# Two adaLN layers on one core: key blocks summed by VectorE ahead of the softmax sums, and a reordered schedule

## The chip, the core and the metric

The kernel runs on one core of a Trainium2 chip. TensorE (PE) does the matrix products, VectorE (DVE), ScalarE (ACT) and GpSimd (POOL) work on tiles, and SyncE (SP) mostly issues DMAs. Each engine has a queue of its own, works through it in order and meets the others through semaphores. The metric is the device time of one execution in microseconds: 575.76 us before, the median of three runs (573.43 to 576.96).

## The reference

Eight batches of 256 tokens with 128 channels go through two layers. Each layer is attention and then a routed feed-forward network, both with a layer norm whose scale and shift come from a small modulation product, and a gate on the way back into the residual:

```
h = _layernorm(x) * (1 + ca) + sa;   x = x + ga * attention(h)
h = _layernorm(x) * (1 + cb) + sb;   x = x + gb * ffn(h)
```

Layer 1, where nearly all of the change lies, has causal attention with 16 heads of width 64. The softmax needs, for each query and head, the sum of the exponentials over the keys. Its feed-forward part has 16 experts with an inner width of 64: sigmoid of the router logits, the best two of each token weighted by their share, and a shared expert besides:

```
out  = einsum('bhst,bhtv->bhsv', softmax(masked / sqrt(64)), v)
ffn  = x + mlp_shared(x) + sum over the two chosen experts of value * mlp_expert(x)
```

## The kernel before

`fast_path` writes every engine's order out by hand. Layer 0 comes first (24 steps of attention, then its experts), then layer 1.

**The loop of layer 1** (L2101 to L2123) has 32 units, four per batch, four heads per unit. Unit n has, in this order: the scores of unit n (L1660), the q and k projections for unit n+2 (L1633), the steps registered for the middle (`at`, list `early`), the value products of unit n-1 (L1681), the v projection for unit n+2 (L1645), and the steps registered for the end (`at_end`, list `ends`). A third list (`at_head`) puts steps between the four heads of the scores. Other work, such as norms, routing, output projections and gathers, is spread over the units through these lists.

**Attention.** A unit's exponentials lie in two tiles `pt` of two heads each, 128 keys by 384 columns: columns 0 to 255 are all 256 queries against the first 128 keys, columns 256 to 383 the second 128 queries against the second 128 keys. ACT makes the exponentials, POOL clears the triangle above the diagonal in four instructions (`causal`, L820), and PE multiplies by v into `o` (L1692). A second group of products (L1700) sums over the keys: its weight is a matrix of ones that sends each head to its own row of `sum`, and it streams all 384 columns, block 0 and then block 1. DVE copies `o` out (L1704). After a batch's last unit DVE takes the reciprocal (L1708), SP sends it through DRAM (`rd`) and back spread over partitions (`rb`), and two units later `normalise1` multiplies (L1725) and `finish1` projects (L1745). The last batch has no such trip: `spread_last` (L1727) spreads the reciprocals with PE.

**Routing.** The rows of the first 12 of the 16 token tiles are scattered by POOL into a sorted DRAM buffer `xs`, in which each of 16 experts has a region. The buffer is cleared first: `z1.clear` (L889) is one DMA of 12 MB, at the end of unit 8. A scatter waits until the buffer is clear (L943). When all rows are placed, `tables_steps` (L956) works out which tile of rows belongs to which expert. Its first step is one small PE product (`cnt`) and fourteen DVE instructions, the last of which gives `widx`, the weights' indices; it runs at the end of unit 29. SP reads these indices into registers and issues the loads: `fetch_weights1` (L1843, groups 4 and up), `find_rows1` (L1839), `fetch_rows1` (L1826). Groups 0 to 3 have fixed places and need no table. The loads of groups 4 and up do.

**After the loop** the ten groups of four tiles go through `turn1` (transpose, L1865), `hidden1` (L1875) and `project_tiles` (L1888), in an order written out from L2128 on. `turn1(m)` issues the rows of group m+4. `project_tiles` leaves its result in two PSUM tiles, which DVE copies to `ysb` (L1899), and SP stores. The PSUM tiles of all this have tags: "s" (two), "o" and "sum" (one each), and "p", which is what `ps_ln` hands out. When the last store has landed, POOL gathers each token's two rows (L1058), and `combine1` adds them, weighted, with PE (L2018). The last 512 tokens instead go densely through all experts (`dense_hidden`, `dense_gate`, `dense_project`), which fills the time of the gathers. `add_h` (L1771, called `add` in the schedule) adds the gated tokens to x on POOL.

Of the kernel before, what the change touches and what calls it, by code (L numbers as in the profile page):

```python
# [9 lines left out]
F32 = mybir.dt.float32  # L10
# [3 lines left out]
ALU = mybir.AluOpType  # L14
AX = mybir.AxisListType

P = 128
# [540 lines left out]
def fast_path(ctx: ExitStack, tc: tile.TileContext, i: dict, out: bass.AP, bad: bass.AP):  # L558
# [302 lines left out]
    class Sorted:  # L861


        def __init__(self, pool, tag, ne, nt, nd):
            self.pool, self.tag, self.ne, self.nt, self.nd = pool, tag, ne, nt, nd
            self.cap = cap = nt * P
            self.placed = 0
            self.scatters = []
            f32 = lambda shape, name: pool.tile(shape, F32, name=f"{name}{tag}")
            self.s12 = f32([P, nt, 2, ne], "s12")  # L870
            self.slot = f32([P, nt, 2], "slot")
            self.region = f32([P, ne], "region")

            self.seen = pool.tile([P, nt + 1, ne], BF16, name=f"seen{tag}")
            self.yidx = pool.tile([P, nt, 2], I32, name=f"yidx{tag}")
            self.rowi = pool.tile([P, nd], I32, name=f"rowi{tag}")
            self.widx = pool.tile([P, nd], I32, name=f"widx{tag}")
            self.xs = dram.tile([ne * cap, P], F32, name=f"xs{tag}")
            self.ys = dram.tile([(ne + nd) * P, P], F32, name=f"ys{tag}")
            nc.gpsimd.tensor_scalar(self.region, num[:, :ne], float(cap), 0.0, ALU.mult, ALU.add)  # L880
            nc.gpsimd.memset(self.seen[:, 0, :], 0.0)
            self.marks = [pool.tile([P, 7, ne], BF16, name=f"marks{tag}{n}") for n in range(E1 // ne)]
            for t in self.marks:
                nc.gpsimd.memset(t[:, 0:3, :], 0.0)
# [1 line left out]
        def tmp(self, shape, name, dt=F32, bufs=2):  # L886
            return self.pool.tile(shape, dt, tag=name, bufs=bufs, name=f"{name}{self.tag}_{self.n}")

        def clear(self, zero):  # L889
            m = zero.shape[1]  # L890
            self.fill = nc.sync.dma_start(
                out=self.xs.rearrange("(p a) c -> p (a c)", p=P).rearrange("p (n m) -> p n m", m=m),
                in_=zero.unsqueeze(1).to_broadcast([P, self.ne * self.cap // m, m]),
            ).ins

        def place(self, *args):
            for _ in self.place_steps(*args):
# [39 lines left out]
        def apart(self, ins):  # L937


            group = f"scatters{self.tag}"  # L940
            if self.scatters:
                tc.declare_no_dep(ins, group=group, reason="different rows")
                tc.add_manual_dep(ins, self.fill.name, WAIT, reason="rows are cleared first")  # L943
            tc.add_to_no_dep_group(group, ins)
            self.scatters.append(ins)

# [445 lines left out]
    def at_end(n, *steps):  # L1392
        ends.setdefault(n, []).extend(steps)
# [66 lines left out]
    first_gates, last_gates = one(gates0(0, 8)), one(gates0(8, 8))  # L1460
    at_end(17, first_gates)
    at_end(18, first_gates)
    at_end(20, first_gates)
    norm6, norm7 = norm0(SPANS0[4]), norm0(SPANS0[5])
    at_end(22, lambda: turn_gates0(0))
    at_end(23, norm6[0], lambda: turn_gates0(1), lambda: ways[SPANS0[3]]())
# [193 lines left out]
    def scores1(b, u, between):  # L1660

        q, k = st1.pop(("q", b, u)), st1.pop(("k", b, u))
        for m in range(2):
# [14 lines left out]
                    step()  # L1678
            st1["pt", b, c] = pt

    def values1(b, u):  # L1681
        v = st1["v", b, u // 2]
        if u == 0:
            st1["s", b] = pp.tile([P, S], F32, tag="sum", bufs=1, name=f"sum1_{b}")
            st1["ou", b] = lp.tile([P, 2, 4, S], F32, tag="ou", name=f"ou1_{b}")
        s = st1["s", b]
        o = pp.tile([P, 2, S], F32, tag="o", bufs=1, name=f"o1_{b}_{u}")
        pts = [st1.pop(("pt", b, 2 * u + m)) for m in range(2)]
        for m in range(2):
            for kb, cols, qs in blocks:  # L1690
                for n in range(2):
                    nc.tensor.matmul(  # L1692
                        out=o[bass.ts(n, D1), m, qs], lhsT=v[:, kb, bass.ts(4 * (u % 2) + 2 * m + n, D1)],
                        rhs=pts[m][:, n, cols], start=(kb == 0), stop=(kb == 1), skip_group_check=True,
                    )

        for kb, cols, qs in blocks:
            for m in range(2):
                for n in range(2):
                    nc.tensor.matmul(  # L1700
                        out=s[bass.ts(2 * n + m, 32), qs], lhsT=on[:, u, :], rhs=pts[m][:, n, cols],
                        start=(kb == 0 and u == 0), stop=(kb == 1 and u == 3), skip_group_check=True,
                    )
        nc.vector.tensor_copy(st1["ou", b][:, :, u, :], o)  # L1704

# [21 lines left out]
    def spread_last(us):  # L1727

        aT = st1["ou", B - 1]
        for u in us:  # L1730
            rp = pp.tile([P, 2, S], F32, tag="s", name=f"rp1_{u}")
            for m in range(2):
                nc.tensor.matmul(
                    out=rp[:, m, :], lhsT=sel[:, u, m].rearrange("p n d -> p (n d)"), rhs=st1["r", B - 1],
                    start=True, stop=True,
                )
            nc.vector.tensor_tensor(aT[:, :, u, :], aT[:, :, u, :], rp, ALU.mult)
# [101 lines left out]
    def find_rows1(m):  # L1839

        starts.extend(z1.row_starts(4 * m - E1, 4))
# [46 lines left out]
    def project_tiles(m):  # L1888
        a = sq.pop(("a", m))
        y = [pp.tile([P, 2, P], F32, tag=tag, bufs=1, name=f"yq1_{m}_{tag}") for tag in ("o", "sum")]  # L1890
        for t in range(4):
            k = t % 2
            nc.tensor.matmul(
                out=y[k][:, t // 2, :], lhsT=a[bass.ts(k, I1), t // 2, :], rhs=weights1(m, t)[2],
                start=True, stop=True,
            )
        ysb = lp.tile([P, 2, 2, P], F32, tag="ysb", bufs=3, name=f"ysb1_{m}")
        for k in range(2):
            nc.vector.tensor_copy(ysb[:, :, k, :], y[k])  # L1899
        nc.sync.dma_start(  # L1900
            out=z1.ys[bass.ds(4 * m * P, 4 * P), :].rearrange("(t p) c -> p t c", p=P),
            in_=ysb.rearrange("p a k c -> p (a k) c"),
        )
# [172 lines left out]
    for bs in ((0, 2), (2, 2), (4, 1), (5, 1)):  # L2076
        n = 4 * sum(bs) + 2
        measure, normalise, modulate, tokens, add = norm1(bs)
        go = one(route1(bs))
        at_end(n, measure)  # L2080
        at(n + 1, normalise)
        at_end(n + 1, modulate, tokens)
        at(n + 2, go)
        at_end(n + 2, go, go, go, go)
        if bs[0] < 5:
            at(n + 4, go)
        else:
            at_end(n + 3, go)
        for k in range(4 * bs[1]):
            if bs[0] < 5:  # L2090
                at_head(n + 5 + k // 2, 1 + 2 * (k % 2), go)
            else:
                at_head(n + 4, 3, lambda go=go: scatter(go, 1))
        if bs[0] < 5:
            at_end(n + 4 if bs[0] else n + 7, add)
    tables = one(z1.tables_steps(ps_ln, True))
    at_end(29, tables, lambda: fetch_weights1(4), lambda: fetch_weights1(5))
    at_end(30, *[lambda m=m: fetch_rows1(m) for m in range(4)], *[lambda m=m: find_rows1(m) for m in range(4, NQ)],
          lambda: fetch_weights1(6))

    for n in range(N):  # L2101
        b, u = divmod(n, 4)
        scores1(b, u, behind.pop(n, {}))
        if n == 0:
            nc.gpsimd.memset(sel, 0.0)
            nc.gpsimd.affine_select(
                out=sel, in_=sel, compare_op=ALU.not_equal, fill=1.0, base=0,
                pattern=[[-8, 4], [-32, 2], [-64, 2], [0, D1]], channel_multiplier=1,
            )
        if n + 2 < N:  # L2110
            project_qk1(*divmod(n + 2, 4))
        for step in early.pop(n, ()):
            step()
        if n:
            values1(*divmod(n - 1, 4))
        if n + 2 < N:
            project_v1(*divmod(n + 2, 4))
        if u == 0 and b:
            reciprocals1(b - 1)
            if b == 2:  # L2120
                z1.clear(zero1)
        for step in ends.pop(n, ()):
            step()  # L2123

# [79 lines left out]
    shared_project(2)  # L2204
    dense_hidden(2)
    dense_hidden(3)
    dense_gate(0)
    dense_hidden(4)
    dense_gate(1)
    dense_hidden(5)  # L2210
    dense_gate(2)
    combine1(0, 1, 2, 3)
    ffn1_add(0)
    dense_hidden(6)
    dense_gate(3)
    dense_project(0)
    dense_project(1)
    dense_hidden(7)
    dense_gate(4)
    combine1(4)  # L2220
    dense_project(2)
    dense_gate(5)
    dense_project(3)
    combine1(5)
    dense_gate(6)
    dense_project(4)
    combine1(6, 7)
    dense_gate(7)
    ffn1_add(1)
    dense_project(5)  # L2230
    combine1(8)
    dense_project(6)
    combine1(9)
    dense_project(7)
    combine1(10, 11)
    ffn1_add(LAST)
    ffn1_add(2)
    manual.close()
    l1.close()
# [94 lines left out]
```

## Time and profile before

| What | Value |
|---|---|
| Runs, median (lowest, highest) | 575.76 us (573.43, 576.96) |
| The profiled execution, own time | 605.03 us |
| Its span, first to last instruction | 603.2 us |
| PE busy, share of the span | 543.5 us, 90% |
| DVE, ACT, POOL busy | 323.8, 265.5, 265.2 us |
| Loop of layer 1 on PE | 239.4 to 493.5 us |
| Granted PE clock, mean | 0.965 |

All times inside the kernel are microseconds from the start of the span of this one profiled execution. It took 29.3 us longer than the median run. Between 545 and 572 us nearly everything but the gathers stands still in it, with waits whose releaser the profile cannot name. "Busy" says little of what bounds a stage. For that one looks at what an engine waited for, and at the chain of work that ended last.

### The profile page before, as it was taken

The numbers are of one execution on the slowest core, as the hardware profiler recorded it, in microseconds if no ns is written. First come the engines' busy times: TensorE is split into PE (matmuls) and PEld (weight loads), VectorE is DVE, ScalarE is ACT, GpSimd is POOL, SyncE is SP. The second block draws the span as 40 slices with busy tenths as digits, with TensorE's granted clock in tenths as the row PEclk, the third lists the DMA queues.
The fourth block names the chain that finished last, engine by engine and source line by source line (L and its number), as shares of the span: only waits on it lengthen the run. The fifth ranks groups of instructions, "written<-read, shape, count | busy, mean of one in ns | idle before, by whom it ended". The sixth has DMA issues, their size and how long they took to land.

```text
span 603.2 us, 12004 instructions
## 1 busy us (share of the span) xinstructions
PE 543.5 (90%) x4499; PEld 384.4 (64%) x4499; DVE 323.8 (54%) x988; ACT 265.5 (44%) x495; POOL 265.2 (44%) x404
## 2 busy tenths in 40 slices
PE   5999998889999998999999989999999989885194
PEld 4355554468999986666767666766767677742064
DVE  4258886666422224655366646558374757771143
ACT  3678775244556633653344423462534322262010
POOL 5224576574444123855123525333563440647400
PEclk9999999799999999999999999999999999987688
DMA  8699100315999713104069831203030355555101
GB/s 278 243 399 406 56 19 27 129 44 155 327 342 354 238 39 153 36 18 99 1 211 408 326 72 46 60 3 71 14 93 10 82 175 170 166 148 131 36 19 57
DMA packets 53566, 85.40 MB, mean 142 GB/s; under 512 B 6652, under 2 KB 32764, under 8 KB 52348
## 3 DMA queue, kind: packets, MB, share of 16 engines
q1 hardware_dynamic: 45308, 60.50, 31.3%
q0 software_dynamic: 8048, 23.67, 12.1%
q8 instruction: 37, 0.61, 0.4%
q10 hardware_dynamic: 144, 0.39, 0.2%
q14 instruction: 29, 0.24, 0.1%
HBM read 53.46 MB, written 31.07 MB: 140 GB/s over the span
## 4 chain that ended last, share of the span: by engine, by line
PE 68%; DVE 12%; DMA 6%; ACT 5%; issue 3%; another core or an unknown queue 3%; SPq 1%; POOL 0%; DVEq 0%; ACTq 0%; POOLq 0%
PE sc L1670 6%; PE hp L1351 6%; PE yt L1359 6%; PE sc L1120 5%; PE o L1692 5%; PE qp L1639 5%; PE y L1745 5%; PE kp L1639 4%; PE vp L1652 4%; PE o L1154 3%; PE sum L1700 3%; DMA rb<-rd 2%; PE gud L1942 2%; DVE ou L1725 2%
## 5 line engine op out<-in xcount | busy, mean ns | idle before, releaser
L822 POOL TENSOR_SCALAR_AFFINE_SELECT pt<-pt 128x256 f32<-128x256 f32 (+1 forms) x144 | 67.1, 494 | 153.8 <-ACT pt L1673 118.3
L1058 POOL DMA_INDIRECT yg<-ys,yidx x56 | 53.9, 963 | 40.7 <-issue 20.5
L1673 ACT ACTIVATE pt<-sc 128x768 f32<-128x768 f32 x64 | 48.4, 808 | 31.2 <-PE sc L1670 31.1
L1136 ACT ACTIVATE pt<-sc 128x1024 f32<-128x1024 f32 x48 | 46.7, 1026 | 24.6 <-PE sc L1120 11.7
L1670 PEld LDWEIGHTS sc<-q,k 64*128 64x128 f32 x512 | 41.6, 187 | 18.7 <-issue 13.8
L1670 PE MATMUL sc<-q,k 64*128 64x256 f32 (+1 forms) x512 | 50.5, 337 | 0.0
L1353 ACT ACTIVATE hst<-hp,wt 128x128 f32<-128x128 f32 x136 | 38.8, 368 | 25.8 <-ACT hst L1353 24.2
L1692 PE MATMUL o<-pt,v 128*64 128x256 f32 (+1 forms) x512 | 48.7, 332 | 1.2 <-DVE ou L1704 1.2
L1655 ACT COPY v<-vp 128x512 f32<-128x512 f32 x32 | 18.7, 585 | 67.4 <-PE vp L1652 67.4
L1050 POOL DMA_INDIRECT wt<-in_wpk_dram,widx x31 | 29.5, 950 | 34.0 <-PE xT L1342 28.3
L1692 PEld LDWEIGHTS o<-pt,v 128*64 128x64 f32 x512 | 31.8, 136 | 18.2 <-issue 5.0
L1643 DVE COPY q<-qp 128x512 f32<-128x512 f32 x32 | 22.0, 688 | 37.3 <-PE qp L1639 37.3
L1364 DVE COPY ysb<-yt 128x128 f32<-128x128 f32 x39 | 11.3, 290 | 49.8 <-PE yt L1359 49.8
L1639 PE MATMUL qp<-h,wq 128*128 128x256 f32 x128 | 36.1, 404 | 1.7 <-DVE sh L1309 1.3
L1120 PE MATMUL sc<-qm,k 32*128 32x512 f32 x192 | 36.0, 722 | 1.4 <-ACT pt L1136 0.8
L1745 PE MATMUL y<-wo,ou 128*128 128x128 f32 x256 | 31.7, 281 | 5.9 <-DVE ou L1725 3.0
L932 POOL DMA_INDIRECT xs<-ht0b,idx x32 | 31.9, 998 | 11.2 <-issue 7.7
L1745 PEld LDWEIGHTS y<-wo,ou 128*128 128x128 f32 x256 | 29.9, 192 | 9.9 <-DVE at L922 4.6
L1652 PE MATMUL vp<-wv,h 128*128 128x512 f32 x64 | 36.0, 645 | 0.0
L1351 PE MATMUL hp<-xTs,wt 128*128 128x128 f32 x272 | 35.9, 275 | 0.0
L1359 PE MATMUL yt<-wt,hst 128*128 128x128 f32 x272 | 35.8, 275 | 0.0
L1351 PEld LDWEIGHTS hp<-xTs,wt 128*128 128x128 f32 x272 | 33.0, 192 | 0.0
(308 smaller groups left out, 1080.9 us busy)
## 6 DMA issues: line engine op xcount, KB each, us to landing
xs<-zero SPq DMA_DIRECT2D x1, 12288.0 KB
xs<-zero SPq DMA_DIRECT2D x1, 8192.0 KB
rb<-rd SPq DMA_DIRECT2D x14, 512.0 KB
mdb<-mrd SPq DMA_DIRECT2D x2, 2048.0 KB
xg<-xs SPq DMA_DIRECT2D x63, 64.0 KB
wt<-in_wpk_dram SPq DMA_DIRECT2D x24, 128.0 KB
wst<-in_wpk_dram SPq DMA_DIRECT2D x5, 514.0 KB
ys<-ysb SPq DMA_DIRECT2D x10, 256.0 KB
```

The costliest lines, as they stand in the source:

```text
L822: nc.gpsimd.affine_select(out=pt, in_=pt, compare_op=ALU.is_ge, fill=0.0, base=0, pattern=[[0, pt.shape[1]], [1, P]], channel_multiplier=-1,)
L1058: nc.gpsimd.indirect_dma_start(out=yg[:, k, :], out_offset=None, in_=self.ys[:, :], in_offset=bass.IndirectOffsetOnAxis(ap=self.yidx[:, j, ...
L1120: nc.tensor.matmul(out=sc[:, n, :].rearrange("p (a q) -> p a q", q=rhs.shape[2]), lhsT=k[r, cols], rhs=rhs, start=True, stop=u < 2,)
L1136: nc.scalar.activation(pt[:, bass.ts(half, 2), :], sc, AF.Exp)
L1351: nc.tensor.matmul(out=hp[:, c, :], lhsT=wt[:, bass.ts(c, P)], rhs=xT, start=True, stop=True)
L1359: nc.tensor.matmul(out=y, lhsT=hs[:, c, :], rhs=wt[:, bass.ds(WF + c * P, P)], start=(c == 0), stop=(c == FC - 1))
L1639: nc.tensor.matmul(out=ps_[:, n, :], lhsT=w1[f"w{what}1"][:, bass.ts(2 * u + n, P)], rhs=hb, start=True, stop=True)
L1652: nc.tensor.matmul(out=vp, lhsT=hb[:, bass.ts(j, P)], rhs=w1["wv1"][:, bass.ts(half, 512)], start=True, stop=True)
L1670: nc.tensor.matmul(out=sc[:, n, cols], lhsT=k[r, m, bass.ts(kb, P)], rhs=q[r, m, qs], start=True, stop=True)
L1673: nc.scalar.activation(pt, sc[:, :, 0:384], AF.Exp, scale=1.0 / math.sqrt(D1))
L1692: nc.tensor.matmul(out=o[bass.ts(n, D1), m, qs], lhsT=v[:, kb, bass.ts(4 * (u % 2) + 2 * m + n, D1)], rhs=pts[m][:, n, cols], start=(kb == ...
L1745: nc.tensor.matmul(out=y[:, j, :], lhsT=aT[:, c % 2, c // 2, bass.ts(j, P)], rhs=w1["wo1"][:, c, :], start=(c == 0), stop=(c == NC1 - 1),)
```

## The change

In layer 1 a new step, `add_blocks1`, follows the v projection of every unit: DVE adds the second key block's 128 columns to the same queries' columns of the first block, for both tiles of the unit. The sums then stream 128 columns of `pt` and 128 columns of the new tile, 256 in place of 384.

The rest moves work. The clearing of `xs` becomes three DMAs at the ends of units 4, 8 and 12. A gate step of layer 0 moves from the end of step 20 to that of 21. `spread_last` takes its PSUM tile from "p". ACT makes the second of the two copies in `project_tiles`. `add_h` of two spans moves a unit later. The rows of groups 0 to 3 are fetched at the end of unit 30, ahead of the tables. The tables' first step moves from the end of unit 29 to the start of unit 31's end steps, and the loads that need it follow in that unit. The dense part after the loop gets another order.

```diff
-        def clear(self, zero):
+        def clear(self, zero, part=0, parts=1):
             m = zero.shape[1]
...
+            n = self.ne * self.cap // m // parts
...
+                for fill in self.fills:
+                    tc.add_manual_dep(ins, fill.name, WAIT, reason="rows are cleared first")
...
-    at_end(20, first_gates)
+    at_end(21, first_gates)
...
+    def add_blocks1(b, u):
+
+        both = st1["both", b, u] = lp.tile([P, 2, 2, P], F32, tag="both", name=f"both1_{b}_{u}")
+        for m in range(2):
+            pt = st1["pt", b, 2 * u + m]
+            nc.vector.tensor_tensor(both[:, m], pt[:, :, P:S], pt[:, :, S : S + P], ALU.add)
...
-        for kb, cols, qs in blocks:
+        both = st1.pop(("both", b, u))
+        for j in range(2):
             for m in range(2):
                 for n in range(2):
                     nc.tensor.matmul(
-                        out=s[bass.ts(2 * n + m, 32), qs], lhsT=on[:, u, :], rhs=pts[m][:, n, cols],
-                        start=(kb == 0 and u == 0), stop=(kb == 1 and u == 3), skip_group_check=True,
+                        out=s[bass.ts(2 * n + m, 32), bass.ts(j, P)], lhsT=on[:, u, :],
+                        rhs=both[:, m, n, :] if j else pts[m][:, n, 0:P],
+                        start=(u == 0 and j == 0), stop=(u == 3), skip_group_check=True,
                     )
...
-            rp = pp.tile([P, 2, S], F32, tag="s", name=f"rp1_{u}")
+            rp = ps_ln([P, 2, S], f"rp1_{u}")
...
-        for k in range(2):
-            nc.vector.tensor_copy(ysb[:, :, k, :], y[k])
+        nc.vector.tensor_copy(ysb[:, :, 0, :], y[0])
+        nc.scalar.copy(ysb[:, :, 1, :], y[1])
...
-            at_end(n + 4 if bs[0] else n + 7, add)
+            at_end(n + 5 if bs[0] else n + 7, add)
     tables = one(z1.tables_steps(ps_ln, True))
-    at_end(29, tables, lambda: fetch_weights1(4), lambda: fetch_weights1(5))
-    at_end(30, *[lambda m=m: fetch_rows1(m) for m in range(4)], *[lambda m=m: find_rows1(m) for m in range(4, NQ)],
-          lambda: fetch_weights1(6))
+    at_end(30, *[lambda m=m: fetch_rows1(m) for m in range(4)])
+    ends[N - 1].insert(0, tables)
+    at_end(
+        N - 1, lambda: fetch_weights1(4), lambda: fetch_weights1(5),
+        *[lambda m=m: find_rows1(m) for m in range(4, NQ)], lambda: fetch_weights1(6),
+    )
...
+        add_blocks1(b, u)
         if u == 0 and b:
             reciprocals1(b - 1)
-            if b == 2:
-                z1.clear(zero1)
+            if b < 4:
+                z1.clear(zero1, b - 1, 3)
...
+    combine1(0, 1, 2, 3)
     dense_gate(0)
-    dense_hidden(4)
     dense_gate(1)
...
     dense_project(0)
     dense_project(1)
+    dense_hidden(4)
...
-    combine1(10, 11)
     ffn1_add(LAST)
+    combine1(8, 9, 10, 11)
     ffn1_add(2)
```

More of the change, by code (lines that the diff above doesn't have):

```diff
@@ L867, in __init__ @@
             self.placed = 0
-            self.scatters = []
+            self.fills, self.scatters = [], []
             f32 = lambda shape, name: pool.tile(shape, F32, name=f"{name}{tag}")
@@ L887, in tmp @@
             return self.pool.tile(shape, dt, tag=name, bufs=bufs, name=f"{name}{self.tag}_{self.n}")
-        def clear(self, zero):
+        def clear(self, zero, part=0, parts=1):
             m = zero.shape[1]
[L891 to L894, printed above, removed]
+            n = self.ne * self.cap // m // parts
+            rows = self.xs.rearrange("(p a) c -> p (a c)", p=P).rearrange("p (n m) -> p n m", m=m)
+            self.fills.append(
+                nc.sync.dma_start(
+                    out=rows[:, bass.ts(part, n), :], in_=zero.unsqueeze(1).to_broadcast([P, n, m])
+                ).ins
+            )
         def place(self, *args):
@@ L942, in apart @@
                 tc.declare_no_dep(ins, group=group, reason="different rows")
-                tc.add_manual_dep(ins, self.fill.name, WAIT, reason="rows are cleared first")
+                for fill in self.fills:
+                    tc.add_manual_dep(ins, fill.name, WAIT, reason="rows are cleared first")
             tc.add_to_no_dep_group(group, ins)
@@ L2094, in fast_path @@
         if bs[0] < 5:
-            at_end(n + 4 if bs[0] else n + 7, add)
+            at_end(n + 5 if bs[0] else n + 7, add)
     tables = one(z1.tables_steps(ps_ln, True))
-    at_end(29, tables, lambda: fetch_weights1(4), lambda: fetch_weights1(5))
-    at_end(30, *[lambda m=m: fetch_rows1(m) for m in range(4)], *[lambda m=m: find_rows1(m) for m in range(4, NQ)],
-          lambda: fetch_weights1(6))
+    at_end(30, *[lambda m=m: fetch_rows1(m) for m in range(4)])
[3 more added lines that the diff above has]
+        *[lambda m=m: find_rows1(m) for m in range(4, NQ)], lambda: fetch_weights1(6),
+    )
     for n in range(N):
@@ L2206, in fast_path @@
     dense_hidden(3)
+    combine1(0, 1, 2, 3)
     dense_gate(0)
-    dense_hidden(4)
     dense_gate(1)
[L2210 to L2215, printed above, removed]
     dense_project(0)
     dense_project(1)
+    dense_hidden(4)
+    dense_gate(2)
+    ffn1_add(0)
+    dense_project(2)
+    dense_hidden(5)
+    dense_gate(3)
+    dense_project(3)
+    dense_hidden(6)
+    dense_gate(4)
+    dense_project(4)
     dense_hidden(7)
-    dense_gate(4)
-    combine1(4)
-    dense_project(2)
     dense_gate(5)
-    dense_project(3)
-    combine1(5)
+    dense_project(5)
+    combine1(4, 5)
     dense_gate(6)
-    dense_project(4)
+    dense_project(6)
     combine1(6, 7)
@@ L2229, in fast_path @@
     ffn1_add(1)
[L2230 to L2233, printed above, removed]
     dense_project(7)
-    combine1(10, 11)
     ffn1_add(LAST)
+    combine1(8, 9, 10, 11)
     ffn1_add(2)
```

## The prediction

> **What bounds the kernel now.** I read the page first, then the stretches, then PE's waits.
>
> ```profile
> span 603.2 us, 12004 instructions
> PE 543.5 (90%) x4499; PEld 384.4 (64%) x4499; DVE 323.8 (54%) x988; ACT 265.5 (44%) x495; POOL 265.2 (44%) x404
> PE 68%; DVE 12%; DMA 6%; ACT 5%; issue 3%; another core or an unknown queue 3%; SPq 1%; POOL 0%; DVEq 0%; ACTq 0%; POOLq 0%
> ```
>
> PE carries 68% of the chain that ended last. The stretches (length, then busy time of PE, PEld, DVE, ACT, POOL, then granted clock) say where:
>
> ```profile
> 103.20:113.40 10.20, 9.36 (x65) 4.42 (x68) 6.21 (x17) 2.83 (x4) 8.99 (x15) 0.50 0.29 92
> 250.00:480.00 230.00, 222.97 (x1901) 155.92 (x1899) 135.35 (x343) 97.38 (x140) 100.32 (x171) 1.00 0.33 100
> 545.00:572.00 27.00, 8.69 (x24) 4.08 (x24) 2.12 (x5) 3.51 (x10) 16.20 (x18) 0.66 0.35 84
> ```
>
> Layer 1's loop is PE-bound: 7 us idle in 230, with DVE at 59%. The third row is a standstill; the execution took 605.03 us (span and 1.8 around it), 29.3 over the median, and I take most of that to sit there. The change touches the work before and behind it, so I form the sum in us against 605.03 and take the same difference from 575.76.
>
> PE's waits:
>
> ```profile
> PE y L1745 <- DVE ou L1725: 3.0, 3, 2.2
> PE y L1745 <- DVE at L922: 2.9, 2, 1.7
> PE yq_o L1893 <- DVE ysb L1899: 2.9, 2, 1.7
> PE gu L1880 <- DVE ou L1737: 1.3, 1, 1.3
> PE o L1692 <- DVE ou L1704: 1.2, 1, 1.2
> ```
>
> **Sums.** PE's order of time around unit 9 (start, length):
>
> ```profile
> 301.01 0.86 PE L1700 MATMUL sum<-pt,on 128*32 128x256 f32 x16
> 301.80 1.13 PE L1652 MATMUL vp<-wv,h 128*128 128x512 f32 x2
> ```
>
> A unit's sums hold PE for 0.79 us. The sixteen are four groups of four side by side. Their single starts are 301.01, 301.25, 301.47 and 301.58: the 256-column groups are 0.24 and 0.22 apart, the 128-column ones 0.11. Four groups of 128 take 0.55, so 0.24 less per unit. I count it for 29 units (30 to 31 wait for something else, below): **-7.0**. If weight loads (sixteen of 0.11, overlapped) set the pace, it is 0; the 0.11 spacing speaks against that.
>
> **The adds** are 64 DVE instructions, 128x256 with two SBUF inputs. The nearest rows:
>
> ```profile
> L1383 DVE TENSOR_TENSOR x<-x,tc 128x256 f32<-128x256 f32 x6 | 2.8, 471 | 0.2
> L1725 DVE TENSOR_TENSOR ou<-ou,rb 128x512 f32<-128x512 f32 x24 | 18.7, 840 | 6.3 <-DMA rb<-rd 6.2
> ```
>
> At 0.45 each they cost DVE 29 us, 0.9 per unit. L1725 alone is 0.68 for twice the columns, but took 1.84 and 1.76 at 415, beside POOL's two-input `add_h`. [...] By the rows only POOL's two-input work does it (beside masks and scatters L818 stays at 0.43), and that is rare. I take 0.45 and keep 0.9 for the range. An add waits for POOL's masks; queued behind it are the end steps and the next q copy. In a common unit the masks end some 3 us into the unit and the add comes 5.6 us in, where DVE idles until the next q. Cover is missing in units with routing: after 404 and 437 DVE runs 9 us on end, and the q copies finish 0.97 and 0.8 us before PE needs them; after 337 they are 0.36 late already. Later reciprocals and shorter PE units add about 0.2 to 0.35 in five such places: **+1.1**.
>
> **Stalls taken away in the loop.** (a) At 353.3 PE waits 2.25 for `rb`: `rd`, behind the 12 MB clearing, took 6.1 us to land at 345, against 2.84 at 439. Split, each third runs 10.3 us (4.2 MB at 410 GB/s) behind its `rb` and is over before the next: **-2.0** (0.2 stays, the q copy and an add being next). The last third ends near 359 on the old scale and may hold unit 15's first scatter, and two masks behind it, 2 us; their values are due 3 us later: 0. (b) `add_h` a unit later leaves L1725 at 0.68 in units 22 and 26. The waits of 1.25 at 420 and 1.70 at 453 go, the second only by 0.6, since `rb` lands late there: **-1.85**. POOL's 2.9 and 1.8 us now delay `ht` in units 23 and 27, under its idle half; uncovered, masks come 1.5 later. (c) Layer 0's gate step is 0.83 us of DVE. It left a place covered by POOL's power (101.64 to 102.36) and comes ahead of `h` at 105.3, which PE awaits: **+0.7** (0 to 0.8).
>
> **The tables.** Here I expect the gain to go. The first step is 5.1 us of DVE (479.31 to 484.42). DVE, POOL and SP in order of time:
>
> ```profile
> 484.17 0.25 DVE L1004 TENSOR_SCALAR widx<-expert_t,wnum_t 128x24 int32<-128x24 f32 x1
> ```
> ```profile
> 487.73 1.47 POOL L822 TENSOR_SCALAR_AFFINE_SELECT pt<-pt 128x256 f32<-128x256 f32 x4
> ```
> ```profile
> 484.97 5.38 SPq L1854 DMA_DIRECT2D wt<-in_wpk_dram  x8
> 490.66 2.05 SPq L1830 DMA_DIRECT2D xg<-xs  x4
> 495.37 1.96 SPq L1854 DMA_DIRECT2D wt<-in_wpk_dram  x4
> ```
>
> SP works without a pause from `widx` to 518.7. In its queue: weights 4 and 5 (5.9), rows 0 to 3 (2.05), six index loads (2.0), weights 6 (2.5), rows 4. Rows 4 are issued from 497.6 to 499.45, and `turn1(4)` finds them just landed: its four transposes from 501.34 take 0.99, against 0.66 elsewhere. Moved, the tables stand behind unit 31's add, which waits for unit 31's masks, which stand behind four scatters on POOL and end near 489.1. `widx` comes near 494.2, 9.8 later. Rows 0 to 3 no longer stand between, and SP needs 2.4+2.4+2.0+2.5 before rows 4: they start near 503.6, not 497.5. PE reaches `turn1(4)` when it did: the 1.15 wait at 485 goes, but transpose 1, `y`'s result and the last reciprocal queue behind the tables on DVE, which brings the first projection back to 498.1. So PE idles about **+6.2**, 0 if SP had slack, 8 if PE gets there early.
>
> A gap that long concerns the clock. After the 12.2 us wait before 572 two dense products took 2.07 and 1.91, until 577.6, and 1.02 from 580: half clock for 5.5 us, 2.7 lost; the 1.15 gap at 485 cost nothing. [...] Some is absorbed by stores SP delays anyway: **+1.5** (0 to 2.7; 5 if it held for 10.2 us as at 103).
>
> **After that.** `rp` in "p" frees hidden group 5 of the 1.31 wait at 513.4, and the router then waits: -1.1. ACT's half of the copies takes 0.33 off DVE per group, but group 8's stands behind eight diagonals of 0.3, holding group 9: +1.4, and DVE runs 1.1 earlier there. Together **-0.8** (-2 to +1.5). At the end, the gated tail of LAST (1.5 us of DVE) hides under 1.8 us of combine, but the first dense projection comes 6 us earlier and meets the gate rows' DMA (issued to 549.8), +0.8: **-0.7** (-1.9 to +0.5).
>
> Sum: -7.0+1.1-2.0-1.85+0.7+6.2+1.5-0.8-0.7 = -2.85. That is 602.2 profiled, and **573 us**.
>
> **Rivals.** *The queue has slack* (0.26): rows 4 arrive in time without the profiler's load, and neither 6.2 nor 1.5 is paid: 565.2. For it: chain and slack are one disturbed execution's. Against: SP is seen busy without a break. *VectorE becomes the bound* (0.14): [...] It decides where the q copy's slack of 0.97 and 0.8 is used up, so in four routing stretches of three units: 12 x 0.94 is 11.3 more, less 2 of slack, giving 582.2. For it: 1.84 at 415. Against: 0.68 in most others. *The sums are no shorter* (0.08), weight loads setting the pace: 580. The forecast itself has 0.47 (569 to 577), and 0.05 is for none of these.
>
> A measurement of this kernel can tell about 1%, 5.8 us, from no change. Faster by more takes the first rival and a tenth of the forecast: 0.30. Slower by more takes two thirds of the second, a third of the third and the unnamed: 0.14. Range 564 to 582: it holds the first rival nearly to its end and the second to its middle.
>
> **What would show it.** Sums at 0.55 per unit; L1725 in units 14, 22, 26 near 0.68 without waits; adds near 0.45; `widx` only after unit 31's masks, PE waiting some 6 us at transpose 4 for `xg`, and a half clock behind it; the router behind `rp`. I am wrong if rows 4 are there in time, if adds take 0.8 or q copies hold PE up, or if the sums stay at 0.79.

## The result and the profile after

The changed kernel took 601.3 us (598.16 to 604.54, four runs) beside 574.6 us for the kernel before (571.46 to 576.96): a ratio of 1.0469, interval 1.039 to 1.0547. It is 26.7 us slower where I had forecast 2.85 us less.

The kernel before takes a different time on different chips: 606.24, 606.63 and 607.27 us (medians) in three of the comparisons below, 576.04 and 575.2 us in two others. The first profile of before (605.03 us), with its standstill at 545 to 572, is like the first sort, the comparison above like the second. So ratios are compared, or kernels that ran side by side, and run E13 gives a profile of the kernel before without the standstill.

The page of the changed kernel, its own time 598.16 us:

```profile
span 596.0 us, 12129 instructions
PE 534.8 (90%) x4499; PEld 383.2 (64%) x4499; DVE 353.0 (59%) x1042; ACT 269.8 (45%) x505; POOL 269.3 (45%) x404
```

The shares hardly differ from before; they don't show the loss. The stretches do (length, then busy time of PE, PEld, DVE, ACT, POOL, then granted clock, DMA share and GB/s). I cut both executions at the same products: the v projection of unit 0, of unit 4 (issued in unit 2), of unit 31 (issued in unit 29), the first shared product behind the experts, and the end. The changed kernel:

```profile
228.38:254.48 26.10, 22.50 (x155) 14.70 (x154) 13.10 (x30) 13.96 (x19) 18.49 (x26) 0.93 0.29 105
254.48:470.71 216.23, 209.13 (x1824) 148.37 (x1820) 149.95 (x368) 92.93 (x133) 95.54 (x158) 1.00 0.32 101
470.71:538.14 67.43, 52.00 (x512) 40.68 (x508) 41.98 (x121) 22.06 (x47) 22.23 (x29) 0.91 0.49 139
538.14:596.00 57.86, 40.10 (x197) 24.80 (x196) 22.60 (x52) 11.81 (x28) 23.75 (x24) 0.85 0.36 89
```

The kernel before in run E13 (575.54 us, span 573.8 us):

```profile
231.44:253.31 21.87, 21.31 (x156) 13.90 (x155) 12.25 (x27) 13.85 (x19) 16.69 (x22) 1.00 0.34 123
253.31:474.34 221.03, 214.95 (x1824) 151.18 (x1820) 125.69 (x322) 92.71 (x133) 93.53 (x163) 0.99 0.33 100
474.34:531.03 56.69, 48.53 (x512) 38.24 (x508) 39.99 (x117) 17.70 (x35) 21.89 (x29) 1.00 0.55 157
531.03:573.80 42.77, 35.11 (x197) 22.16 (x196) 22.60 (x53) 12.47 (x30) 23.08 (x24) 0.90 0.50 124
```

| Stretch | Before | After | Difference |
|---|---|---|---|
| Start and layer 0 | 231.44 | 228.38 | -3.1 |
| First units | 21.87 | 26.10 | +4.2 |
| Rest of the loop | 221.03 | 216.23 | -4.8 |
| Last units, experts | 56.69 | 67.43 | +10.7 |
| Dense tail | 42.77 | 57.86 | +15.1 |

The sum is the difference of the spans, 22.2. The first row isn't the change's: by layer 0's second v projection, up to which both versions have the same work, the changed kernel is 3.75 us ahead (24.74 against 28.49 us), and another execution of it (E5) has 28.24 there. So the loop as a whole gives 0.6 where I had counted 9.75, and the end costs 25.8.

PE's waits in the changed kernel (total, times, longest):

```profile
PE of L1965 <- DVE a L1960: 9.6, 5, 2.0
PE xT L1882 <- DMA xg<-xs: 4.8, 1, 4.8
...
PE xT L1882 <- DVE t L1764: 3.4, 1, 3.4
...
PE qp L1643 <- DVE h L784: 2.6, 1, 2.6
PE yq_sum L1906 <- ACT ysb L1912: 2.4, 1, 2.4
PE kp L1643 <- DVE h L784: 2.3, 2, 1.2
```

The `y <- ou` and `y <- at` waits are no longer among the first. In their place stand a dense projection that waits for its gate product (five times), `turn1(4)` that waits for its rows (`xg`), and DVE and ACT in other places. A piece of the chain that ended last shows the first of them (start, length, what):

```profile
569.85 1.73 PE gud L1955 x4
571.59 0.02 issue
571.61 0.61 ACT a L1949
572.21 0.02 issue
572.24 0.04 DVE a L1950
...
572.84 0.70 DVE a L1960
573.54 0.04 issue
573.58 1.97 PE of L1965 x8
```

Hidden part, silu, its product, then a gate product, then a projection, one after the other. But the gate product of 572.84 belongs to the hidden part two before (`dense_hidden(6)` is issued just ahead of `dense_gate(4)`). It doesn't need the silu of 571.61. It only stands behind that silu's product in DVE's queue.

### The profile page after: what moved, and what is told of

It is laid out like the page before. It is cut to its first block, busy times and chain, and to the rows that moved or that the text cites. A ratio compares the mean times of both kernels' runs of the same rounds, so it can differ in the third digit from the quotient of the medians.

```text
span 596.0 us, 12129 instructions
## 1 busy us (share of the span) xinstructions
PE 534.8 (90%) x4499; PEld 383.2 (64%) x4499; DVE 353.0 (59%) x1042; ACT 269.8 (45%) x505; POOL 269.3 (45%) x404
## 3 DMA queue, kind: packets, MB, share of 16 engines
q0 software_dynamic: 8048, 23.67, 12.2%
## 5 line engine op out<-in xcount | busy, mean ns | idle before, releaser
L822 POOL TENSOR_SCALAR_AFFINE_SELECT pt<-pt 128x256 f32<-128x256 f32 (+1 forms) x144 | 69.2, 508 | 147.2 <-ACT pt L1677 115.7
L1062 POOL DMA_INDIRECT yg<-ys,yidx x56 | 55.8, 997 | 42.8 <-DMA ys<-ysb 20.4
L1677 ACT ACTIVATE pt<-sc 128x768 f32<-128x768 f32 x64 | 48.4, 808 | 26.5 <-PE sc L1674 25.5
L1690 DVE TENSOR_TENSOR both<-pt 128x256 f32<-128x256 f32 x64 | 33.4, 558 | 9.2 <-POOL pt L822 9.2
L1643 PE MATMUL kp<-h,wk 128*128 128x256 f32 x128 | 34.0, 389 | 2.3 <-DVE h L784 2.3
L1647 ACT COPY k<-kp 128x512 f32<-128x512 f32 x32 | 18.8, 587 | 37.1 <-PE kp L1643 37.1
```

The source lines that it names most:

```text
L822: nc.gpsimd.affine_select(out=pt, in_=pt, compare_op=ALU.is_ge, fill=0.0, base=0, pattern=[[0, pt.shape[1]], [1, P]], channel_multiplier=-1,)
L1062: nc.gpsimd.indirect_dma_start(out=yg[:, k, :], out_offset=None, in_=self.ys[:, :], in_offset=bass.IndirectOffsetOnAxis(ap=self.yidx[:, j, ...
L1643: nc.tensor.matmul(out=ps_[:, n, :], lhsT=w1[f"w{what}1"][:, bass.ts(2 * u + n, P)], rhs=hb, start=True, stop=True)
L1647: copy(st1[what, b, u], ps_)
L1677: nc.scalar.activation(pt, sc[:, :, 0:384], AF.Exp, scale=1.0 / math.sqrt(D1))
```

## The experiments

No kernel here leaves work out.

**The parts undone.** E1 and E2 put the tail's and the tables' order back into the changed kernel, E3 both; E4 puts the new tail alone into the kernel before. The edit of the tail is the block from `dense_hidden(3)` to the end, in the order of the diff above; that of the tables:

```diff
-    at_end(30, *[lambda m=m: fetch_rows1(m) for m in range(4)])
-    ends[N - 1].insert(0, tables)
-    at_end(N - 1, lambda: fetch_weights1(4), ...)
+    at_end(29, tables, lambda: fetch_weights1(4), lambda: fetch_weights1(5))
+    at_end(30, ...)
```

> The changed kernel with the dense tail in its old order. Theory (order of the tail): with each gate product queued on VectorE behind the product of the hidden part just issued, TensorE waits 2.0 us in front of five projections (9.6 us in the profile of the changed kernel) and 1.6 us for the gates, some 12 us in all: about 589 us against 601. Rival (a hold-up of some 25 us in the tail, as the profile of the kernel before has it at 545 to 572, now also falls on the timed runs, whatever the order): about 601 us, with such a gap in its profile. Second rival (the tables alone cost it all): 601 us.

> The changed kernel with the tables and the fetches of the experts' weights at units 29 and 30 as before. Theory (tables moved to the last unit cost the start of the experts): between unit 31 and the first shared product the changed kernel lost some 9 us against the one before (from 6.3 us ahead at unit 31's values to 5.6 us behind, of which some 3 us are its other waits): about 591 us. Rival (only the tail counts): 601 us. Rival (the transfers only wait elsewhere): 598 to 601 us.

> The changed kernel with both the tail and the tables as before; what stays are the sums by added blocks, the split fill, the gate step and the additions one unit later, the router products in the other buffer and the ScalarE copy. Theory (tail and tables are independent and carry the loss): about 579 us, within 1% of before; the rest brings nothing, since the units gain 0.2 us each and lose it again at waits. Rival (they hide one behind the other): 585 to 590 us. Rival (the added blocks carry a part of the loss): over 585 us. If the rest gains as forecast: 568 to 572 us.

> The kernel before with the new order of the dense tail alone. Theory (order of the tail): 575 + 12 = 587 us. Rival (the loss needs the tables' delay, or a hold-up that has nothing to do with the order): 575 us.

The kernel before took 606.24 us here, so the expected microseconds don't hold and the ratios count: E1 1.0172 (1.0124 to 1.0221), E2 1.0307 (1.0247 to 1.0367), E3 1.0076 (1.0054 to 1.0099), E4 1.0136 (1.0043 to 1.0228). All four profiles have the near-standstill in the tail. So it is no answer to the question of the loss: it comes with this chip, with the old and the new order alike. Against the changed kernel's 1.0418 on another such chip (E5, below) the old tail takes off 2.5%, the old tables 1.1%. What E3 leaves, 0.76% slower, was a surprise: with tail and tables undone, the sums and the small edits should have gained about 10 us.

**The parts alone.** E5 is the changed kernel beside the parts, E6 the additions and shorter sums alone, E7 the small edits (split clearing, gate step, `add_h` a unit later, `rp` in "p", ScalarE's copy), E8 the tables alone.

> The changed kernel as it is, beside the parts. Theory (the parts add up): 1.0469 of the kernel before as in the first measurement; on a chip where the kernel before takes 606 us that is some 634, where it takes 575 us some 602. Rival (the loss is tied to the chip of the first measurement): a ratio under 1.03.

> The kernel before with the added blocks and the shorter sums alone. My forecast's terms: 7.0 us less for the sums and 1.1 us more for waits on VectorE: 1.0% faster. Theory now (the additions hold up VectorE's queue in front of what TensorE waits for, at the layer norms, the modulated blocks and the last unit; from the profile of the changed kernel with both old parts some 12 us): 0.8% slower, with the units at 6.52 us for 6.73, and 2 to 3 us lost each at units 2 to 3, 13 and 25. Rival (the loss of that kernel comes from the other small edits): 1% faster.

> The small edits alone (split fill, gate step one unit later, additions one unit later, router products in the other buffer, ScalarE copy), with sums, tables and tail as before. Forecast's terms: -2.0 -1.85 +0.7 -0.8 = 4 us or 0.7% faster. Theory now (the added blocks cost it): 0.5 to 0.8% faster. Rival (the small edits carry the loss): 0.5% slower or worse.

> The kernel before with the tables and the fetches of the experts at the last unit. Forecast's term: +6.2 us and 1.5 us for the clock: 1.3% slower. Rival (without the additions VectorE is free to build the tables at once, and the transfers are in time): within 0.5%. Rival (they cost more as they also hold the last corrections): 2% slower.

Measured: E5 1.0418 (1.0356 to 1.0479), E6 1.0116 (1.0078 to 1.0154), E7 0.993 (0.9904 to 0.9956), E8 1.0103 (1.0073 to 1.0132); the kernel before took 606.63 us. E6 is slower as the new theory said, though somewhat more; E7 and E8 are near what the forecast's own terms had. In E8 PE waits at `turn1(4)`:

```profile
PE xT L1869 <- DMA xg<-xs: 4.5, 1, 4.5
```

That is the wait of the forecast, on `xg`, with no other change in the program. E8 and E6 stretch the time from unit 31's v projection to the shared products by 5.4 and 5.3 us against the first profile of before (61.24 and 61.16 for 55.86); the changed kernel has both, +10.7.

How the additions lose is read in E6. PE's waits at 235 to 265 us, where the first profile of before has only one of 0.4:

```profile
PE qp L1639 <- DVE h L784: 2.6, 1, 2.6
PE vp L1652 <- DVE q L1643: 1.0, 1, 1.0
```

And DVE in order of time there (the bracket is the idle time and what ended it), first E6, then before:

```profile
255.58 0.42 DVE L1686 TENSOR_TENSOR both<-pt 128x256 f32<-128x256 f32 x1 [2.55 <-POOL pt L822]
255.92 0.54 DVE L784 TENSOR_SCALAR h<-nt1a,md 128x256 f32<-128x256 f32 x1
```
```profile
251.12 0.68 DVE L1704 COPY ou<-o 128x512 f32<-128x512 f32 x1
251.72 0.53 DVE L784 TENSOR_SCALAR h<-nt1a,md 128x256 f32<-128x256 f32 x1
```

The addition of 0.42 us isn't long. It stands at the head of DVE's queue for 2.55 us, until POOL has masked its tile, and the modulated block `h`, whose input is there, stands behind it with PE waiting. From the v projection of unit 0 to that of unit 4 E6 needs 26.7 us, the first profile of before 21.7; the granted clock of 251.0 to 262.2 us is 0.85 in E6.

**The additions one unit later.** E9 adds in front of the products that use the sums, where the masks are long done; E11 is E9 with the small edits, E12 that with the tail of E10.

```diff
         if n:
+            add_blocks1(*divmod(n - 1, 4))
             values1(*divmod(n - 1, 4))
...
-        add_blocks1(b, u)
```

> The kernel before with the shorter sums, but the additions are issued one unit later, in front of the products that use them, when the masks are done and the norm's work is ahead of them in VectorE's queue. Theory (an addition waits for GpSimd's mask at the head of VectorE's queue and holds the modulated block and the copies behind it): the losses at units 0 to 3, 13 and 25 go and the 0.21 us of each unit stay: 0.7 to 1.1% faster than before, 600 to 602.5 us where before takes 606.6. Rival (the additions cost by their own 0.45 us each, wherever they stand, or by GpSimd's slower masks): 0.5 to 1.2% slower as with the additions in their unit.

> The small edits (split fill and the others) with the late additions and the shorter sums; tables and tail as before. If the parts add up: 3.2 us and 4 to 6 us less than before, 596 to 600 us, 1.1 to 1.7% faster. Rival (the late additions hold the values' copies and the gain of the sums goes there): 0.5% faster as the small edits alone.

> The same with the new tail and its gate products ahead. Theory: within 2 us of the same kernel with the old tail. Rival (the new order has a gain of its own once the wait is gone, as my forecast had it at 0.7 us): 1 to 3 us less.

The theory's remedy fell: E9 1.0874 (1.0809 to 1.0939), E11 1.0931 (1.0889 to 1.0973), E12 1.0866 (1.0821 to 1.0911). E12's interval overlaps E11's, so the tail makes no clear difference here. E11, PE's waits and PE around 320 us:

```profile
PE sum L1712 <- DVE both L1690: 44.9, 21, 4.6
```
```profile
316.14 0.43 PE L1712 MATMUL sum<-pt,on 128*32 128x128 f32 x8
321.15 0.95 PE L1712 MATMUL sum<-both,on 128*32 128x128 f32 x8 [4.58 <-DVE both L1690]
```

DVE made this addition only at 320.68, right behind a norm that had waited for ScalarE until 317.02 and the four multiplications of `ou`. Here the norm holds up the addition instead of the addition the norm, and PE itself waits for it, 21 times in all. Of the two orders neither is free: DVE's queue is in order, and the place that is right in one unit is wrong in another.

**The gate products ahead.** E10 keeps the new tail but swaps four pairs of lines, so that DVE has the gate product before the next hidden part's product:

```diff
-    dense_hidden(4)
     dense_gate(2)
+    dense_hidden(4)
     ffn1_add(0)
     dense_project(2)
-    dense_hidden(5)
     dense_gate(3)
+    dense_hidden(5)
...
```

> The kernel before with the new tail, but each gate product is issued ahead of the hidden part that stood in front of it; all else of the new order stays. Theory (the gate product behind the next hidden part's product in VectorE's queue makes TensorE wait 2.0 us in front of each of five projections): 10 us less than with the new tail, within 0.5% of before, 604 to 609 us. Rival (the corrections' products put ahead of the projections, or the last corrections at the very end, cost it): 613 to 620 us as with the new tail.

It measured 1.0106 (1.0062 to 1.0151), above the 0.5% that I had allowed, and on another chip than E4. So the pair was run again side by side, E14 the new tail and E15 the swapped one, with E13, the kernel before, for its profile.

> The kernel before, for its profile on the chip of the runs beside it. Both theories of the tail need it where the gap of 545 to 572 is absent: if the kernel before takes about 575 us here, its tail (first shared product to the end) should be about 45 us with no gap over 5 us; if it takes about 606 us, some 65 us with the gap.

> The new tail alone once more, on one chip with the next run. Theory (gate products behind the next hidden part's product): 1.4 to 2.1% slower than before. Rival (the first value of 1.4% belongs to that chip's gap): under 1%.

> The new tail with the gate products ahead, beside the new tail. Theory: 6 to 10 us less than the new tail; what stays over before (some 5 us by the last measurement) lies with the corrections' place. Rival (the queue's order is not what costs): within 3 us of the new tail.

E13 took 575.54 us with no standstill: its tail is 42.77 us, its longest wait of PE there 0.5. E14 is 1.0305 (1.0231 to 1.038), more than the 1.4 to 2.1% expected; E15 is 1.0083 (1.0053 to 1.0113): the swap takes off 2.2%, 12.8 us, where 6 to 10 were expected. The first row of PE's waits in the tail, E13, E14 and E15:

```profile
PE good_cnt L2029 <- DVE whole L2026: 0.5, 1, 0.5
```
```profile
PE of L1952 <- DVE a L1947: 9.6, 5, 2.0
```
```profile
PE of L1952 <- DVE a L1947: 2.6, 3, 1.6
```

The 9.6 us are those of the changed kernel to the tenth, and 7.0 of them go with the order of DVE's queue alone. Most of the rest is the clock. The tails as a whole, E14 and E15:

```profile
528.42:588.20 59.78, 41.25 (x197) 24.81 (x196) 22.68 (x53) 12.46 (x30) 23.08 (x24) 0.85 0.37 88
```
```profile
532.04:577.80 45.76, 34.11 (x197) 21.90 (x196) 22.79 (x53) 12.36 (x30) 23.03 (x24) 0.97 0.47 116
```

Of 14.0 us between these two executions, 6.9 are idle time of PE and 7.1 the same 197 products at a lower granted clock. Some 1.7 of the 7.1 lie at the tail's start, where E14, like E13, is at half clock and E15 isn't. The others follow the waits. In E14 the third of the five waits ends at 558.82:

```profile
552.70:556.10 3.40, 2.17 (x11) 1.57 (x12) 2.47 (x4) 0.00 (x0) 2.71 (x3) 1.00 0.23 61
556.10:559.50 3.40, 1.39 (x8) 0.68 (x7) 1.29 (x2) 0.60 (x1) 2.57 (x3) 1.00 0.49 137
559.50:562.90 3.40, 3.40 (x9) 1.60 (x7) 0.00 (x0) 0.00 (x0) 2.15 (x3) 0.50 0.17 39
```

PE is busy for 1.39 us of the middle row and makes nothing for 2.0, and then the clock is halved. The fourth and fifth waits are followed by 3.4 us at half clock too, the first two aren't. What E15 keeps above before, 0.8%, has one wait of 1.6 us that the old order lacks: the first projection waits for the gates' transfer, where the old order has two more hidden parts to issue. The rest of the 0.8% isn't traced.

**The additions only where nothing waits behind them.** E16 has the small edits and the additions in 21 units; E18 leaves units 28 and 29 out as well; E17 is E7 once more, beside E18.

```diff
+    QUIET = {*range(3, 10), *range(12, 18), *range(20, 26), 28, 29}
...
+        if n in QUIET:
+            add_blocks1(b, u)
```

> The small edits, tables and tail as before, and the added blocks with the shorter sums only in 21 of the 32 units, those in which no norm, correction or table stands in VectorE's queue behind an addition. Theory (the loss of the added blocks is made in the other units): 21 x 0.21 = 4.4 us less than the small edits alone (0.993): 0.984 to 0.989. Rival (the additions cost in every unit, by GpSimd's masks or VectorE's load): 0.993 to 1.0.

> The small edits alone once more, beside the next run: 0.990 to 0.996 of before, as measured (0.993).

> The small edits with the added blocks in 19 quiet units, without units 28 and 29, whose additions in the profile of the 21-unit form push the tables of the last 1.7 us back. Theory (the sums gain 0.21 us in each unit where nothing waits behind the additions): 19 x 0.21 = 4.0 us less than the small edits alone: 0.984 to 0.988 of before. Rival (the additions' gain goes later in any case): within 1 us of the small edits alone.

E16 is 0.9933 (0.9911 to 0.9955), not the 0.984 to 0.989 of the theory; E17 0.9939 (0.9913 to 0.9964), E18 0.9912 (0.988 to 0.9944). E18 has the lowest ratio measured here and beats the kernel before and the changed one, but against E17 its intervals overlap: a gain of the sums themselves (1.7 us between the medians, 4.0 expected) isn't established. In E18's profile the quiet units are 6.52 us for 6.73. Of what they gain, 1.5 us goes back around unit 24 (10.92 from one v projection to the next, 9.38 in E17), where a projection then waits 1.4 us for a routing step on DVE.

## Why the prediction was wrong

The parts measured alone, in us of the kernel before beside them, against the terms of my sum:

| Part | Forecast | Measured |
|---|---|---|
| Sums and additions | -7.0 +1.1 | +7.0 (E6) |
| Small edits | -2.0 -1.85 +0.7 -0.8 | -4.2 (E7), -3.7 (E17) |
| Tables | +6.2 +1.5 | +6.2 (E8) |
| Dense tail | -0.7 | +17.5 (E14), +8.2 (E4) |

With E14 the measured ones add up to 26.5, the whole to 26.7. That agreement is partly luck: E6 to E8 ran on a chip with the standstill and E14 on one without. With E4 they add up to 17.2, where the changed kernel on E6's chip (E5) is 25.4 over before. Two terms failed, the sums with their additions by 13 us and the tail by 18.

**The tail is the first step that failed.** I costed "the gated tail of LAST (1.5 us of DVE)" and when the first dense projection would come, and gave it -0.7. I looked at when each input is there and never followed DVE's queue through the new order. There `dense_gate(p)` stands behind the product of `dense_hidden(p+2)`, which needs a silu, which needs a product that PE is only about to make. So every projection pays a trip through PE, ACT and DVE: 1.73, 0.61, then DVE's products in the chain above, with PE idle for 2.0 us of it. In the old order mostly two or three later gate products stand between a gate product and its projection, with other products for PE, and E13 pays no such wait. E15 against E14 shows it for 12.8 of the 17.5 us; since the edit changes nothing but that order, this is shown and not argued. The other 4.7 are E15's 0.8%. Of the 15.1 us between the stretches, 10.1 are idle time of PE (17.76 for 7.66) and 5.0 the same 197 products at a lower clock (40.10 for 35.11).

**The additions are the second.** The direct half was right. The sums' groups are 128 columns, the units 6.52 us where nothing else happens. The additions, from the view of their line (minimum, median and maximum in ns; below, what ended DVE's idle time before them, in us and times):

```profile
L1690 DVE TENSOR_TENSOR both<-pt x64: 410/420/1492, 235.9 to 484.1; 128x256 f32<-128x256 f32 x64
...
  POOL pt L822: 9.2, 6
```

Median 0.42 for my 0.45. What I called "+1.1" for waits behind later q copies was mis-sized, for three reasons. First, "queued behind it are the end steps and the next q copy" is in the prediction, but I priced the q copy alone. `h` in the first units is such an end step, and E6 loses 5.0 us there. The second row has DVE idle for 9.2 us with an addition at the head of its queue, six times, until POOL's masks are done. Second, additions slow down beside POOL's work, which I had kept for the range alone. In the changed kernel 18 of the 64 additions begin while POOL computes, and 17 of these end 0.28 to 0.29 us after POOL's instruction does. So 13 of the 64 take over 0.6, up to 1.49: ten beside POOL's two-input products, three, at 0.62, beside masks. The 29 that overlap no work of POOL stay under 0.45. DVE and POOL at 325 us:

```profile
325.40 2.55 DVE L1690 TENSOR_TENSOR both<-pt 128x256 f32<-128x256 f32 x2
327.88 0.53 DVE L784 TENSOR_SCALAR h<-nt1b,md 128x256 f32<-128x256 f32 x1
```
```profile
324.97 1.29 POOL L1781 TENSOR_TENSOR ht<-xn1b,mdb 128x512 f32<-128x512 f32 x1 [0.32 <-DVE xn1b L766]
326.34 1.33 POOL L1782 TENSOR_TENSOR ht<-ht,mdb 128x512 f32<-128x512 f32 x1
```

POOL's two products have two SBUF inputs each, and beside them two additions take 2.55 us for 0.84, again with an `h` behind them. At this place and at its like of 391 us PE then waits 1.2 us for `h` (the last row of its waits above), and from one v projection to the next the changed kernel needs 9.8 us, E13 8.6 and 8.7. My reading, that beside masks L818 stays at 0.43, was wrong in the first profile already: beside a mask it took 0.51 at 339.54. The collisions with POOL's two-input work are at six places, as few as I thought, but four of them are a norm's, where DVE can least spare the time. Third, I counted no effect in units 30 and 31 since they "wait for something else". E6 shows +5.3 us from there to the end of the experts: the additions stand among the tables' steps, and the last batch's value products wait 2.9 us for DVE in place of 1.2.

**The tables** were sized about right alone: 6.2 for 7.7. The changed kernel shows the forecast's signs, `widx` behind unit 31's additions at 490.33 and `turn1(4)` late (idle 4.83 for "some 6"), but also one that I had named and not priced. DVE and PE there:

```profile
483.13 1.89 DVE L1690 TENSOR_TENSOR both<-pt 128x256 f32<-128x256 f32 x2 [2.31 <-POOL pt L822]
...
490.33 0.24 DVE L1008 TENSOR_SCALAR widx<-expert_t,wnum_t 128x24 int32<-128x24 f32 x1
490.48 0.42 DVE L1764 TENSOR_TENSOR t<-y,mdb 128x256 f32<-128x256 f32 x1
```
```profile
490.95 0.66 PE L1882 MATMUL xT<-ident,xg 128*128 128x128 f32 x4 [3.40 <-DVE t L1764]
...
503.43 1.89 PE L1882 MATMUL xT<-ident,xg 128*128 128x128 f32 x4 [4.83 <-DMA xg<-xs]
```

At `turn1(1)` PE idles 3.40 us for `t`, behind the tables' whole run on DVE. In E8, where no addition stands ahead of that run, the same wait is 0.35. The four transposes of 503.43 take 1.89 us for 0.66, since the clock is halved behind the gap:

```profile
503.40:508.80 5.40, 5.25 (x33) 3.72 (x34) 1.07 (x6) 1.31 (x3) 0.00 (x0) 0.50 0.45 129
```

What the lower clock cost here I estimate at half of these 5.25 us, some 2.6. My +1.5 was an estimate too: the first profile had a gap of 1.15 us that cost nothing and one of 12.2 us that cost 2.7, and none of about 5. Shorter waits were followed by half clock too, but not each time: the one of 3.40 us above, in E14's tail three of the four of 2.0 us, in the changed kernel's tail the two of 2.01 us that end at 573.58 and 580.13, but not the two that end at 563.80 and 568.69. The changed kernel from 491.9, then its tail:

```profile
491.90:495.20 3.30, 3.30 (x32) 2.97 (x29) 2.14 (x3) 2.16 (x4) 0.00 (x0) 0.50 0.63 199
```
```profile
562.00:573.50 11.50, 5.75 (x24) 3.14 (x24) 5.13 (x8) 1.62 (x3) 7.81 (x8) 1.00 0.28 76
573.80:577.10 3.30, 3.30 (x11) 2.27 (x11) 0.00 (x0) 0.00 (x0) 0.00 (x0) 0.50 0.00 0
577.20:580.10 2.90, 0.92 (x3) 0.09 (x1) 1.31 (x3) 0.60 (x1) 0.00 (x0) 1.00 0.01 3
580.60:583.90 3.30, 3.30 (x18) 3.30 (x17) 0.68 (x2) 0.00 (x0) 0.00 (x0) 0.50 0.01 2
```

From what length on a wait brings half clock, these profiles don't show.

**The small edits** have the right sum by luck, since their terms miss in both directions. In E17 against the first profile of before, the stall for `rb` at 353 is gone, -2.7 for "-2.0" from one v projection to the next. (That stretch is 13.2 to 15.5 us long in the seven profiles compared with one clearing, 10.1 to 10.9 in nine with three, so that 2.7 is at the low end.) `add_h` a unit later leaves the multiplications at 0.69 us but gives nothing: 1.5 us gained between two v projections, 1.9 lost before the one after. ScalarE's copy stands behind eight diagonals as I had feared, and PE waits 2.4 us for it. From unit 31's v projection to the shared products E17 needs 57.67 us for 55.86, and 56.69 in E13: 1.0 to 1.8 more where I had -0.8. Whether the gate step of layer 0 cost its +0.7 the profiles can't tell; kernels with the same layer 0 differ by up to 7 us there.

**The rivals.** That the queue has slack is refuted by E8, that the sums are no shorter by the units of 6.52 us. That VectorE becomes the bound, by additions of 0.9 us beside POOL, an estimate of twice the 0.45, has part of the truth: ten of the 64 took 0.94 to 1.49. But the point was a norm's `h` and not the slack of the q copies. None of my cases had the tail, so the range ended 19 us below the result. That the standstill at 545 to 572 lay outside the timed runs was right for the runs of the forecast. It stays open what it waits for, and why the new tail alone cost 8.2 us with it (interval 2.6 to 13.8) and 17.5 without. Taking it away wasn't tried.

## What to carry to other kernels

Where each engine works through its queue in order, read a reordered block once per engine: for every instruction that a later stage needs, look at what stands directly in front of it and what that one is waiting for. A short instruction that waits for a third engine passes its wait on to all that queues behind it (2.55 us for the addition of 0.42 in E6), so price an added VectorE step by its releaser and not by its own 0.4 us. And measure parts apart: here edits worth 0.7% were buried under three that cost 1.0, 1.2 and 3.1%.

## What the runs showed of the hardware

- The same kernel took 575 us on some chips and 606 us on others. Its tail is 70.3 us in the first profile of before and 42.8 in E13, 27.5 of the difference. In the 30 us of the 24 gathers PE made 60 products in the first and 174 in the second, with POOL as busy in both:

```profile
536.60:566.40 29.80, 15.72 (x60) 6.96 (x56) 6.12 (x19) 5.29 (x13) 22.77 (x24) 0.79 0.54 122
```
```profile
534.80:564.90 30.10, 29.29 (x174) 19.31 (x171) 17.40 (x37) 8.71 (x19) 23.07 (x24) 1.00 0.58 134
```

- In E14's tail the granted clock went to half for 3.4 us after waits of 2.0 us, three times of the four, and the same 197 products held PE 7.1 us longer than in E15's. In the changed kernel's tail it did so twice of four, and behind the wait of 4.83 us it stayed at half to 508.8.
- Additions of 128x256 with two SBUF inputs took 0.42 us alone, about 0.62 at three places beside POOL's masks and 0.94 to 1.49 where they were slowest, always beside POOL's two-input products. Of the 18 that began while POOL computed, 17 ended 0.28 to 0.29 us after POOL's instruction.
- The late additions cost more than the early ones (8.7% for 1.2%), though their inputs were long there.
